# Twelve more key gathers of a GRU/AUGRU kernel wait for a state of the recurrence before they are issued

## The chip, the cores and the metric

The kernel runs on one core of a Trainium2 chip. A core has a matrix engine (TensorE, PE in the profile), a vector engine (VectorE, DVE), an activation engine (ScalarE, ACT), a general engine (GpSimd, POOL) and an engine that mostly issues DMAs (SyncE, SP). Each works through its own list of instructions in order and meets the others only through semaphores. GpSimd also issues the indirect DMAs, the gathers by a list of row numbers. Time is the device time of one launch in microseconds (us).

## The reference

A batch of 1024 users has a history of T = 100 items each, with 128 numbers per item, all in float32. A GRU runs over the history and leaves 100 keys per user. An attention network scores every key against the item in question, with a softmax over the unmasked ones. A second recurrence (AUGRU) runs over the keys again; its update gate is scaled by an attention value. The state at each user's own length goes through a small network to one number. The AUGRU is where the change lies:

```python
def augru_step(h, inp):
    x_t, a_t = inp
    ti = jnp.concatenate([h, x_t], axis=-1)
    r = sigmoid(ti @ aug_Wr.T + aug_br)
    u = sigmoid(ti @ aug_Wu.T + aug_bu)
    h_hat = tanh(concatenate([h * r, x_t], axis=-1) @ aug_Wh.T + aug_bh)
    u = a_t[:, None] * u
    h_new = (1.0 - u) * h + u * h_hat
    return (h_new, h_new)
_, aug_seq = scan(augru_step, h0, (swapaxes(keys, 0, 1), att_seq))
attention_feature = take_along_axis(aug_out, idx, axis=1)[:, 0, :]   # idx = length - 1
```

## The kernel before

**Two phases.** The first phase runs the GRU with the attention and the pooling beside it (`gru_phase`, up to about 1400 us of the profile). The second, `augru_phase`, runs the AUGRU over t = 1 to 99. State 0 is worked out at the end of the first phase.

**Two halves.** The users are sorted by length and split into two halves of 512 (i = 0 and i = 1), features on the 128 partitions and users along the free dimension. Users whose sequence has ended drop out, so the columns shrink from 510 at t = 1 to 500 at t = 3, 496 at t = 4 and so on. `half_step(t, i)` does one step of one half, and the halves alternate: while VectorE and ScalarE finish one half, TensorE works on the other.

**One half step.** TensorE first closes the gate ph of the half step before with its r (L1268), then the gates pr and pu of this half step with the state h (L1268), and then opens three gates of the next half step with its keys (L1264: pr, ph, pu). Each is two matmuls. ScalarE takes the sigmoids (L1292, L1293) and the tanh (L1276). VectorE does pu·c (L1298), r = h·pr (L1300), the new h (L1302), pu·attention (L1305) and `rest` = (pu - 1)·h (L1308). `rest` lives in a ring of three buffers.

**The keys.** The first phase stores the keys in HBM in the order of the users as given; the AUGRU needs them in sorted order. They are fetched by gathers on GpSimd (L193 in `load_row`): one gather brings the keys of 32 sorted users for eight steps, 128 rows of 256 numbers, and sixteen gathers bring a half. `READ` splits the steps into stretches: 0 to 3 (stretch 0), then stretches of eight from `FIRST` = 4, 12, 20 and on. `load_key` turns gathered rows into a matmul operand: by TensorE and ScalarE for stretch 0 (L1246, L1247), by VectorE's transposes for the later ones (L1253).

**When gathers are issued.** The rows of stretch 1 for the first half are fetched during the first phase. For the second half, four of sixteen gathers are issued ahead of the loop and the other twelve by the list `due`, three after each of the four half steps of t = 1 and t = 2. From t = 3 on the gathers of stretch 2 and later are spread in the same way. The place in the program alone doesn't hold GpSimd back, since its list runs ahead of the others. What does is `later["pace"]`: where it is set, `load_row` first copies one column of that tensor into the gather's destination (L192), so that the copy waits for the tensor and the gather for the copy. After `half_step` it is a column of `rest`, and in the kernel before it is left empty for t = 1 and t = 2 (`SOON` is 4).

Ahead of these gathers in GpSimd's list stand eight gathers of pooled attention rows (`att_r`, L158).

Of the kernel before, what the change touches and what calls it, by code (L numbers as in the profile page):

```python
# [58 lines left out]
SOON = P // R  # L59
# [26 lines left out]
def kernel(ctx: ExitStack, tc: tile.TileContext, a: dict, out: bass.AP):  # L86
# [67 lines left out]
    later = {}  # L154
# [998 lines left out]
    def augru_phase(pools, widths, alive):  # L1153
# [22 lines left out]
        def bank(name, n=None):  # L1176

            if n is None:
                n = ring.pop(0)
                ring.append(n)  # L1180
            return ps[n].tile([P, HB], F32, tag="g", name=name)
# [7 lines left out]
        def chosen_rows(i, p, lhsT):  # L1189
            nc.tensor.matmul(p, lhsT=lhsT, rhs=chosen[i], start=True, stop=True)  # L1190

        def first_weights(i, p):
            at = att[1, i] = wp.tile([P, HB], F32, name="at", bufs=6)
            nc.scalar.copy(at, p)

        def store_chosen(i, p):
            chosen_rows(i, p[:SOON, :], quad)
            rows_t = wp.tile([P, HB], F32, tag="att_t", name="att_t", bufs=2)
            nc.scalar.copy(rows_t[:SOON, :], p[:SOON, :])
            nc.sync.dma_start(out=att_d[i][:SOON], in_=rows_t[:SOON, :])  # L1200
            for t in range(2, SOON):
                load_att(t, i)

        def mask_weights(i):
            later_rows = sorted_rows[i][:, :, SOON:T]
            nc.vector.tensor_mul(later_rows, later_rows, used_s[:, i])

        def store_weights(i):

            n = T - SOON  # L1210
            p = pa.tile([P, HB], F32, tag="a", name="pw")
            for g in range(GH):
                nc.tensor.transpose(p[:n, ts(g, P)], sorted_rows[i][:, g, SOON:T], ident)
            rows_t = wp.tile([P, HB], F32, tag="att_t", name="att_t", bufs=2)
            nc.vector.tensor_copy(rows_t[:n, :], p[:n, :])
            nc.sync.dma_start(out=att_d[i][SOON:], in_=rows_t[:n, :])
            load_att(SOON, i)

        def load_att(t, i):
            w = widths[t]  # L1220
            if t >= one and i:
                at = att.pop((t, 0))
            else:
                at = wp.tile([P, HB], F32, name="at", bufs=6)
            att[t, i] = at
            if t >= one:
                at = at[:, ts(i, P)]
            nc.sync.dma_start(
                out=at[:, :w], in_=att_d[i][t, :w].partition_broadcast(P)
            )  # L1230

        def load_key(t, i):

            q = max(j for j, first in enumerate(FIRST) if first <= t)
            w, m, r = widths[t], t - FIRST[q], rows[q, i]
            if t >= one and i:
                k = keys.pop((t, 0))
            else:
                k = qp.tile([P, HB], F32, name="k3")
            keys[t, i] = k  # L1240
            if t >= one:
                k = k[:, ts(i, P)]
            if q < WHOLE:
                p = pa.tile([P, HB], F32, tag="a", name="pk3")
                for g in range(-(-w // P)):
                    nc.tensor.transpose(p[:, ts(g, P)], r[:, g, ts(m, P)], ident)  # L1246
                nc.scalar.copy(k[:, :w], p[:, :w])  # L1247
            else:
                w, n = -(-w // R), KH // len(r)
                for j, part in enumerate(r):  # L1250
                    u = min(w - j * n, n)
                    if u > 0:
                        nc.vector.transpose(  # L1253
                            k.rearrange("p (k r) -> p k r", r=R)[:, j * n : j * n + u, :],
                            part[:, :u, ts(m, R)],
                        )

        def open_gates(t, i, names=("pr", "ph", "pu"), banks=(None,) * 3):

            k = keys[t, i][:, : widths[t]]  # L1260
            for name, n in zip(names, banks):
                m = {"pr": wr, "ph": wh, "pu": wu}[name]
                p = opened[t, i, name] = bank(name, n)[:, : widths[t]]
                nc.tensor.matmul(p, lhsT=m[:, 1, :], rhs=k, start=True, stop=False)  # L1264

        def close_gate(t, i, name, m, v):
            p = opened.pop((t, i, name))
            nc.tensor.matmul(p, lhsT=m[:, 0, :], rhs=v, start=False, stop=True)  # L1268
            return p

        def open_state(t, i):

            r, u, rest = resets.pop((t, i))
            ph = close_gate(t, i, "ph", wh, r)
            c = wp.tile([P, HB], F32, name="c3")[:, : widths[t]]
            nc.scalar.activation(c, ph, AF.Tanh, bias=later["bh"])  # L1276
            states[i] = u, c, rest, h3[i][:, : widths[t]]

        def half_step(t, i):


            w, h = widths[t], h3[i][:, : widths[t]]
            before, after = ((t - 1, 1), (t, 1)) if i == 0 else ((t, 0), (t + 1, 0))
            if before in resets:
                open_state(*before)
            pr = close_gate(t, i, "pr", wr, h)
            pu = close_gate(t, i, "pu", wu, h)
            if t == 1:
                row = pa.tile([P, HB], F32, tag="a", name="row")
                chosen_rows(i, row, quad[:, 1:2].to_broadcast([P, P]))  # L1290
                open_gates(1, i, ("ph",), (None, LATE_BANKS[2])[1 - i :])
            nc.scalar.activation(pr, pr, AF.Sigmoid, bias=later["br"])  # L1292
            nc.scalar.activation(pu, pu, AF.Sigmoid, bias=later["bu"])  # L1293
            if t == 1:
                first_weights(i, row)
            state = states.pop(1 - i, None)
            if state is not None:
                nc.vector.tensor_mul(state[0], state[0], state[1])  # L1298
            r = wp.tile([P, HB], F32, name="r3")[:, :w]
            nc.vector.tensor_mul(r, h, pr)  # L1300
            if state is not None:
                nc.vector.tensor_sub(state[3], state[0], state[2])  # L1302
            if (t, i) == (1, 1):
                store_chosen(0, bank("spare", SPARE))
            nc.vector.tensor_mul(pu, pu, att.pop((t, i))[:, :w])  # L1305
            rest = wp.tile([P, HB], F32, name="rest")[:, :w]

            nc.vector.scalar_tensor_tensor(  # L1308
                out=rest, in0=pu, scalar=1.0, in1=h, op0=ALU.subtract, op1=ALU.mult
            )  # L1310
            later["pace"] = rest[:, 0:1] if t > SOON - 2 else None
            resets[t, i] = r, pu, rest
            if t == 2:
                mask_weights(i)
            if t == 1:
                load_key(2, i)
            if (t, i) == (1, 0):
                open_gates(1, 1, ("pr", "pu"))
            elif after[0] < min(T, one) and (*after, "pr") not in opened:
                open_gates(*after)  # L1320
            elif after[0] == one < T:
                open_both(one, "pr", "pu", "ph")
            if (t, i) == (1, 1):
                store_chosen(1, pa.tile([P, HB], F32, tag="a", name="spare"))
                load_key(3, 0)
            elif (t, i) == (2, 0):
                load_key(3, 1)
            elif (t, i) == (2, 1):
                store_weights(0)
            elif (t, i) == (3, 0):  # L1330
                store_weights(1)
            if SOON - 2 < t < T - 2:
                load_att(t + 2, i)

            if t == FIRST[1] - 1:
                load_key(t + 1, i)
            if (t, i) == (FIRST[1], 1):
                load_key(t + 1, i)
            if FIRST[1] - 2 < t < T - 2 and (t, i) != (FIRST[1] - 1, 1):
                load_key(t + 2, i)  # L1340
# [5 lines left out]
        def open_both(t, *names):  # L1346

            w = widths[t]
            for name in names:
                p = opened[t, name] = bank(name)  # L1350
                m = {"pr": wr, "ph": wh, "pu": wu}[name]
                nc.tensor.matmul(
                    both(p, w), lhsT=m[:, 1, :], rhs=both(keys[t, 1], w, P),
                    start=True, stop=False,
                )
# [233 lines left out]
        if one < T:  # L1589
            next(final)  # L1590
            c, rest, h = sums.pop(T - 1)
# [108 lines left out]
```

## Time and profile before

| what | us |
|---|---|
| median of 3 runs | 1998.83 (1998.15 to 1998.97) |
| the profiled execution, its own time | 2015.4 |
| its span, first to last instruction | 2013.5 |
| TensorE busy with matmuls | 1982.8 |
| VectorE busy | 1674.2 |
| GpSimd busy | 1262.1 |
| ScalarE busy | 940.4 |

The profile is of one execution, which isn't one of the timed runs. In the rows of a timeline the columns are the start in us, the duration in us, the engine, the line of the kernel, the operation, the output and its inputs, the shape, the count, and in brackets how long the engine had been idle and what it waited for. In a row of windows the numbers after the stretch and its length are the busy time of PE, PEld (weight loads), DVE, ACT and POOL, then the granted TensorE clock (1.00 is full), the share of the DMA engines and GB/s. The ends of matmuls are modelled, and the starts are recorded.

### The profile page before, as it was taken

What the parts mean: (1) busy time and instruction counts of PE and PEld (TensorE: products, weight loads), DVE (VectorE), ACT (ScalarE), POOL (GpSimd) and SP (SyncE); (2) the same over time, 40 slices, a digit from 0 to 9 for tenths busy, and PEclk for the clock granted to TensorE, in tenths of its full rate; (3) what the DMA queues carried; (4) which work ended last, traced back from release to release, by engine and by line L of the source; (5) the groups of instructions that cost most, each with busy time, mean ns of one, the idle gap of its engine ahead of it and who ended that gap; (6) DMA issues with size and microseconds to landing.
All of it is one profiled execution on the core that took longest, in us unless ns stands there. A gap on an engine that the chain in (4) does not pass through costs nothing.

```text
span 2013.5 us, 40927 instructions
## 1 busy us (share of the span) xinstructions
PE 1982.8 (98%) x15324; PEld 875.7 (43%) x15324; DVE 1674.2 (83%) x3036; ACT 940.4 (47%) x1689; POOL 1262.1 (63%) x1300
## 2 busy tenths in 40 slices
PE   9999999999999999999999999999699999999998
PEld 2333333333333333333333333334244556678997
DVE  7888998887888897888888898998477777888885
ACT  4445444444445454445445454455234444445553
POOL 0333939569796959495987767989553354445331
PEclk9999999999999999999999999999899999999999
DMA  4443333323334334333432333332443333333331
GB/s 124 98 117 100 98 107 107 105 84 90 107 115 108 108 117 122 109 115 105 126 101 80 99 107 92 107 107 83 126 136 93 95 110 98 94 104 95 81 81 35
DMA packets 244572, 205.59 MB, mean 102 GB/s; under 512 B 61811, under 2 KB 207068, under 8 KB 244364
## 3 DMA queue, kind: packets, MB, share of 16 engines
q1 hardware_dynamic: 231852, 170.31, 29.9%
q0 software_dynamic: 12224, 32.05, 5.7%
q8 instruction: 122, 2.00, 0.4%
q14 instruction: 86, 0.70, 0.1%
q10 hardware_dynamic: 288, 0.52, 0.1%
HBM read 146.75 MB, written 54.42 MB: 100 GB/s over the span
## 4 chain that ended last, share of the span: by engine, by line
PE 93%; DVE 2%; POOL 2%; another core or an unknown queue 1%; ACT 1%; issue 1%; DMA 0%; SPq 0%; DVEq 0%; ACTq 0%; POOLq 0%
PE ps L588 48%; PE pm L770 17%; PE ph L1268 4%; PE pr L1268 4%; PE pu L1268 4%; PE ph L1264 4%; PE pr L1264 4%; PE pu L1264 4%; POOL pooled L700 1%; PE last L737 1%; POOL kw L699 1%; PE pr L1359 0%; PE ph L1359 0%; POOL hist L574 0%
## 5 line engine op out<-in xcount | busy, mean ns | idle before, releaser
L588 PE MATMUL ps<-x,wih 128*32 128x512 f32 x4800 | 601.9, 592 | 0.0
L588 PE MATMUL ps<-hn,whh 128*32 128x512 f32 x4752 | 596.8, 592 | 0.0
L588 PEld LDWEIGHTS ps<-x,wih 128*32 128x32 f32 x4800 | 174.4, 110 | 342.6 <-issue 337.9
L588 PEld LDWEIGHTS ps<-hn,whh 128*32 128x32 f32 x4752 | 172.8, 110 | 339.1 <-issue 337.0
L600 ACT ACTIVATE r<-ps,brz 128x512 f32<-128x512 f32 x200 | 137.5, 687 | 381.9 <-PE ps L588 381.7
L573 POOL TENSOR_TENSOR xm<-x,m 128x512 f32<-128x512 f32 x200 | 233.5, 1168 | 66.9 <-DMA m<-mask_d 66.6
L574 POOL TENSOR_TENSOR hist<-hist,xm 128x512 f32<-128x512 f32 x200 | 257.7, 1288 | 15.7
L193 POOL DMA_INDIRECT rows<-keys_d,idx_k x218 | 211.9, 972 | 85.2 <-POOL rows L192 49.7
L700 POOL TENSOR_TENSOR pooled<-pooled,kw 128x512 f32<-128x512 f32 x192 | 245.0, 1276 | 15.0
L699 POOL TENSOR_TENSOR kw<-kt,e 128x512 f32<-128x512 f32 x192 | 206.3, 1074 | 69.0 <-DVE e L888 69.0
L621 ACT ACTIVATE ps<-ps,bih 128x512 f32<-128x512 f32 x198 | 131.1, 662 | 229.8 <-DVE ps L618 228.7
L770 PE MATMUL pm<-hn,wk 128*32 128x512 f32 x1200 | 214.9, 592 | 0.0
L770 PE MATMUL pm<-kq,wkq 128*32 128x512 f32 x1200 | 214.8, 592 | 0.0
L1276 ACT ACTIVATE c<-ph,bh 128x510 f32<-128x510 f32 (+57 forms) x174 | 88.1, 506 | 254.5 <-PE ph L1268 222.1
L608 DVE SCALAR_TENSOR_TENSOR u<-ps,bhh,r 128x512 f32<-128x512 f32 x198 | 147.5, 745 | 68.8 <-PE ps L588 66.6
L770 PE MATMUL pm<-mv,w 128*32 128x512 f32 (+1 forms) x808 | 194.9, 592 | 1.0 <-DVE e L869 1.0
L192 POOL COPY rows<-rest 128x1 f32<-128x1 f32 x186 | 34.9, 188 | 209.5 <-DVE rest L1308 205.5
L631 DVE TENSOR_TENSOR d<-hn,ps 128x512 f32<-128x512 f32 x198 | 136.1, 687 | 35.9 <-ACT ps L621 35.5
L618 DVE TENSOR_TENSOR ps<-ps,u 128x512 f32<-128x512 f32 x200 | 140.0, 700 | 25.2 <-remote 4.1
L632 DVE TENSOR_TENSOR d<-ps,d 128x512 f32<-128x512 f32 x198 | 136.9, 691 | 26.1 <-ACT ps L622 11.1
L642 ACT COPY hn<-ps 128x512 f32<-128x512 f32 x198 | 115.5, 583 | 91.6 <-DVE kq L637 89.9
L1298 DVE TENSOR_TENSOR pu<-pu,c 128x510 f32<-128x510 f32 (+57 forms) x173 | 81.8, 473 | 89.7 <-ACT c L1276 62.9
(271 smaller groups left out, 3141.3 us busy)
## 6 DMA issues: line engine op xcount, KB each, us to landing
x<-in_hist_x SPq DMA_DIRECT2D x210, 256.0 KB
keys_d<-kt SPq DMA_DIRECT2D x48, 1024.0 KB
m<-mask_d SPq DMA_DIRECT2D x200, 128.0 KB
rows<-keys_d,idx_k POOLq DMA_INDIRECT x218
s_b<-mv SPq DMA_DIRECT2D x200, 8.0 KB
keys_d<-kt SPq DMA_DIRECT2D x32, 64.0 KB
mask_i<-in_mask SPq DMA_DIRECT2D x8, 200.0 KB
part_d<-part SPq DMA_DIRECT2D x2, 400.0 KB
```

The lines of the kernel that those rows point to most:

```text
L193: nc.gpsimd.indirect_dma_start(out=r[:, at, :], out_offset=None, in_=keys_d[q], in_offset=bass.IndirectOffsetOnAxis(ap=idx_k[:, k, i : i + ...
L573: nc.gpsimd.tensor_mul(d, x, m)
L574: nc.gpsimd.tensor_add(acc, acc, d)
L588: nc.tensor.matmul(p[ts(q, R), :], lhsT=w[:, g, ts(q, R)], rhs=v, start=(j == 0), stop=(j == len(parts) - 1),)
L600: nc.scalar.activation(r, pr, AF.Sigmoid, bias=brz[:, 0:1])
L608: nc.vector.scalar_tensor_tensor(out=u, in0=ph, scalar=bhh[:, 2:3], in1=r, op0=ALU.add, op1=ALU.mult,)
L618: nc.vector.tensor_add(pi, pi, u)
L699: eng.tensor_mul(d, k, w)
L700: eng.tensor_add(acc, acc, d)
L770: nc.tensor.matmul(p[i][s, :], lhsT=w[:, s], rhs=v, start=start, stop=stop)
L1264: nc.tensor.matmul(p, lhsT=m[:, 1, :], rhs=k, start=True, stop=False)
L1268: nc.tensor.matmul(p, lhsT=m[:, 0, :], rhs=v, start=False, stop=True)
```

## The change

The exception for t = 1 and t = 2 is taken out:

```diff
@@ half_step @@
             nc.vector.scalar_tensor_tensor(
                 out=rest, in0=pu, scalar=1.0, in1=h, op0=ALU.subtract, op1=ALU.mult
             )
-            later["pace"] = rest[:, 0:1] if t > SOON - 2 else None
+            later["pace"] = rest[:, 0:1]
             resets[t, i] = r, pu, rest
```

On GpSimd the place is the run of sixteen gathers behind the att_r gathers (`rows_14796` is their destination, `keys_d1` the HBM tensor of stretch 1; DMASW names are semaphores of the gathers). Before, they stand one behind the other:

```order
L158 DMA att_r_14791<-pooled_d_80,idx_88 128x128 [waits DMASW7_49]
L193 DMA rows_14796<-keys_d1_61,idx_k_89 128x256 [waits DVE_49,DMASW0_49,PE_49,Activation_49]
L193 DMA rows_14796<-keys_d1_61,idx_k_89 128x256 [waits DMASW1_49]
L193 DMA rows_14796<-keys_d1_61,idx_k_89 128x256 [waits DMASW2_49]
L193 DMA rows_14796<-keys_d1_61,idx_k_89 128x256 [waits DMASW3_49]
L193 DMA rows_14796<-keys_d1_61,idx_k_89 128x256 [waits DMASW4_49]
L193 DMA rows_14796<-keys_d1_61,idx_k_89 128x256 [waits DMASW5_49]
```

In the changed kernel the same place reads (`rest_14814` is that of step 1, first half, `rest_14860` that of step 1, second half):

```order
L193 DMA rows_14796<-keys_d1_61,idx_k_89 128x256 [waits DMASW3_49]
L192 COPY rows_14796<-rest_14814 128x1 [waits DVE_49]
L193 DMA rows_14796<-keys_d1_61,idx_k_89 128x256 [waits DMASW4_49,Pool_49]
L192 COPY rows_14796<-rest_14814 128x1
L193 DMA rows_14796<-keys_d1_61,idx_k_89 128x256 [waits DMASW5_49,Pool_49]
L192 COPY rows_14796<-rest_14814 128x1
L193 DMA rows_14796<-keys_d1_61,idx_k_89 128x256 [waits DMASW6_49,Pool_49]
L192 COPY rows_14796<-rest_14860 128x1 [waits DVE_49]
L193 DMA rows_14796<-keys_d1_61,idx_k_89 128x256 [waits DMASW7_49,Pool_49]
```

The first four gathers stay as they are; each of the other twelve has a copy ahead of it, three copies for each of the four half steps.

On VectorE the place is the half step of t = 3, second half, where the gathered rows are first used. Before:

```order
L1305 TENSOR_TENSOR pu_14974<-pu_14974,at_14879 128x500 [waits DMAHW2_49,Activation_49]
L1308 SCALAR_TENSOR_TENSOR rest_15013<-pu_14974,h_all_93 128x500 [waits DVE_49]
L1253 STREAM_TRANSPOSE k3_15023<-rows_14796 128x512 [waits DMASW4_49,DMASW5_49,DMASW3_49,DMASW6_49,DMASW2_49,DMASW7_49,DMASW1_49,DMASW0_49]
L1298 TENSOR_TENSOR pu_14974<-pu_14974,c3_15030 128x500 [waits Activation_49]
L1300 TENSOR_TENSOR r3_15037<-h_all_93,pr_15015 128x496 [waits Activation_49]
```

And in the changed kernel:

```order
L1305 TENSOR_TENSOR pu_14986<-pu_14986,at_14882 128x500 [waits DMAHW2_49,Activation_49]
L1308 SCALAR_TENSOR_TENSOR rest_15025<-pu_14986,h_all_93 128x500 [waits DVE_49,Pool_49]
L1253 STREAM_TRANSPOSE k3_15035<-rows_14796 128x512 [waits DMASW4_49,DMASW3_49,DMASW5_49,DMASW2_49,DMASW6_49,DMASW1_49,DMASW7_49,DMASW0_49,Pool_49]
L1298 TENSOR_TENSOR pu_14986<-pu_14986,c3_15042 128x500 [waits Activation_49]
L1300 TENSOR_TENSOR r3_15049<-h_all_93,pr_15027 128x496 [waits Activation_49]
```

The order is the same. L1308 and L1253 also wait for GpSimd: L1308 because its buffer is one that copies have read (the same new wait stands at the L1308 of t = 2, second half, and t = 3, first half), L1253 because the copies write into its input. Apart from this no instruction of any engine has moved.

## Prediction

> **What bounds the kernel now.** I read the page first: which engine is full, and what the chain that ended last consists of.
>
> ```profile
> PE 1982.8 (98%) x15324; PEld 875.7 (43%) x15324; DVE 1674.2 (83%) x3036; ACT 940.4 (47%) x1689; POOL 1262.1 (63%) x1300
> PE 93%; DVE 2%; POOL 2%; another core or an unknown queue 1%; ACT 1%; issue 1%; DMA 0%; SPq 0%; DVEq 0%; ACTq 0%; POOLq 0%
> ```
>
> TensorE sets the time. Work on another engine costs nothing until TensorE has to wait for it, and then it costs the wait. Only 2013.5 - 1982.8 = 30.7 us of the span are without a matmul. So I looked next at the timeline of the AUGRU's first steps, where the changed gathers stand, TensorE first:
>
> ```profile
> 1432.64 0.60 PE L1246 MATMUL pk<-ident,rows 128*128 128x128 f32 x4
> ...
> 1436.46 1.00 PE L1264 MATMUL ph<-k,wh 128*128 128x500 f32 x2
> 1447.14 2.04 PE L1264 MATMUL pu<-k,wu 128*128 128x500 f32 x2 [9.68 <-issue]
> ...
> 1453.43 2.05 PE L1268 MATMUL ph<-r,wh 128*128 128x506 f32 x2 [3.40 <-DVE r L1300]
> ...
> 1458.49 1.00 PE L1264 MATMUL pr<-k,wr 128*128 128x500 f32 x2
> 1459.33 1.00 PE L1264 MATMUL ph<-k,wh 128*128 128x500 f32 x2
> ...
> 1463.96 0.99 PE L1264 MATMUL pr<-k,wr 128*128 128x496 f32 x2
> ```
>
> This is the largest hole of the profiled execution, and it lies just beside the changed gathers. From an opening of ph to the next opening of pr, half a step on, the undisturbed rows need 1463.96 - 1459.33 = 4.63 us. So after the ph at 1436.46 the pr of step 3, second half, was due at 1441.09; it came at 1458.49. The hole costs 17.4 us: 9.68 + 3.40 of waiting, the rest by a slow clock. On ScalarE one sees what was late:
>
> ```profile
> 1430.29 0.66 ACT L1293 ACTIVATE pu<-pu,bu 128x506 f32<-128x506 f32 x1
> 1442.90 0.57 ACT L1247 COPY k<-pk 128x500 f32<-128x500 f32 x1 [11.95 <-remote]
> 1446.41 0.68 ACT L1276 ACTIVATE c<-ph,bh 128x506 f32<-128x506 f32 x1 [2.93 <-remote]
> 1452.00 0.66 ACT L1292 ACTIVATE pr<-pr,br 128x506 f32<-128x506 f32 x1 [4.92 <-remote]
> ```
>
> The copy at 1442.90 waits for the transposes of 1432.64 alone, which by their row end at 1433.24. It started 9.7 us after that. The next two were late in the same way, so that the bank for pu came free late. No gather is an input of these three instructions. Now the times: the profiled execution took 2015.4 us, the median of the runs is 1998.83, 16.6 less. Without the hole only 30.7 - 13.1 = 17.6 us without matmuls are left in the whole span, start and tail included, and nearly all of it would have to vanish to make 16.6. The hole itself, 17.4, fits. I therefore read it as belonging to the recorded execution and not to the timed ones, and lay out the timed schedule by taking 17.4 us off every row behind it.
>
> [...]
>
> **The change part by part.** GpSimd's own rows, before and after the hole:
>
> ```profile
> 1428.34 0.94 POOL L158 DMA_INDIRECT att_r<-pooled_d,idx  x1 [0.30 <-issue]
> 1429.58 0.95 POOL L193 DMA_INDIRECT rows<-keys_d,idx_k  x1 [0.30 <-issue]
> ...
> 1433.33 0.95 POOL L193 DMA_INDIRECT rows<-keys_d,idx_k  x1 [0.30 <-issue]
> 1434.58 0.95 POOL L193 DMA_INDIRECT rows<-keys_d,idx_k  x1 [0.30 <-issue]
> ...
> 1448.34 0.94 POOL L193 DMA_INDIRECT rows<-keys_d,idx_k  x1 [0.30 <-issue]
> 1460.99 0.18 POOL L192 COPY rows<-rest 128x1 f32<-128x1 f32 x1 [11.71 <-DVE rest L1308]
> 1461.71 0.98 POOL L193 DMA_INDIRECT rows<-keys_d,idx_k  x1 [0.53 <-POOL rows L192]
> 1462.69 0.20 POOL L192 COPY rows<-rest 128x1 f32<-128x1 f32 x1
> 1463.16 0.98 POOL L193 DMA_INDIRECT rows<-keys_d,idx_k  x1 [0.27 <-POOL rows L192]
> 1464.14 0.19 POOL L192 COPY rows<-rest 128x1 f32<-128x1 f32 x1
> ```
>
> - *How many.* The first four of the sixteen gathers are issued ahead of the loop, when there is no state to wait for. Twelve change, from the one at 1434.58 on.
> - *The waits.* The copies wait, three each, for the state rows (rest) of steps 1 and 2:
>
> ```profile
> 1416.23 0.69 DVE L1308 SCALAR_TENSOR_TENSOR rest<-pu,h_all 128x510 f32<-128x510 f32 x1
> 1421.53 0.69 DVE L1308 SCALAR_TENSOR_TENSOR rest<-pu,h_all 128x510 f32<-128x510 f32 x1
> 1432.11 0.69 DVE L1308 SCALAR_TENSOR_TENSOR rest<-pu,h_all 128x506 f32<-128x506 f32 x1
> ...
> 1454.82 0.69 DVE L1308 SCALAR_TENSOR_TENSOR rest<-pu,h_all 128x506 f32<-128x506 f32 x1
> ...
> 1460.15 0.68 DVE L1308 SCALAR_TENSOR_TENSOR rest<-pu,h_all 128x500 f32<-128x500 f32 x1
> ```
>
> GpSimd is held back by the eight att_r gathers and is free for the first changed copy at 1434.3. By then the first three states are there (1416.9, 1422.2, 1432.8). The fourth, recorded at 1454.82 + 0.69 = 1455.5, is due at 1438.1 without the hole, and its copies come up after nine gathers, at about 1447. So in the timed runs no copy waits: this part costs 0.
> - *The copies themselves.* With no wait, a gather with its copy goes from 1461.71 to 1463.16, 1.45 us; without one, (1448.34 - 1429.58)/15 = 1.25. Twelve times 0.20 is 2.4 us more on GpSimd. At the upper end each group's first copy costs what it does behind a real wait (1460.99 to 1461.71, 0.72, for 0.47), four times 0.25, and the delay is 3.4. I take 2.4, since nothing is waited for.
> - *When the rows land.* The last gather ends its issue at 1449.28. In the DMA view of 1448 to 1452 us (forty slices of 0.1 us) the last traffic is in the slice from 1450.6:
>
> ```profile
> DMA  3000000958567000000299426610000000000000
> ```
>
> So the sixteenth lands at about 1450.7 now, and at 1450.7 + 2.4 = 1453.1 after the change.
> - *Who needs them.* VectorE transposes all sixteen at once for step 4, second half, and TensorE opens that step's gates with the result:
>
> ```profile
> 1466.03 0.68 DVE L1308 SCALAR_TENSOR_TENSOR rest<-pu,h_all 128x500 f32<-128x500 f32 x1
> 1466.76 0.71 DVE L1253 STREAM_TRANSPOSE k<-rows 128x512 f32<-128x512 f32 x1
> 1468.20 0.69 DVE L1298 TENSOR_TENSOR pu<-pu,c 128x500 f32<-128x500 f32 x1 [0.73 <-ACT c L1276]
> 1469.00 0.67 DVE L1300 TENSOR_TENSOR r<-h_all,pr 128x496 f32<-128x496 f32 x1
> ...
> 1468.95 0.99 PE L1264 MATMUL pr<-k,wr 128*128 128x496 f32 x2
> ...
> 1471.45 0.99 PE L1268 MATMUL ph<-r,wh 128*128 128x496 f32 x2
> ```
>
> The transpose ended at 1467.47, 1.48 us ahead of its matmul. Taking 17.4 off, it would start at 1449.36 and could start as late as 1449.36 + 1.48 = 1450.84 before TensorE waits. Now the rows land at 1450.7, just inside: before, the wait of VectorE is covered. At 1453.1 they are 1453.1 - 1450.84 = 2.3 us late, and TensorE is idle for that. Behind the transpose in VectorE's queue stand the product for h, r and h of step 4; r was done at 1469.67 for a ph at 1471.45, and since the opened gates shift as well, this adds nothing to the 2.3.
> - *The new wait on VectorE.* Three of the L1308 now wait until GpSimd has copied from the buffer that they overwrite (a ring of three). The last copies of the first three states end, at 1.45 each from 1434.3, at 1437.4, 1441.7 and 1446.1. The L1308 of (2,1), (3,0) and (3,1) are due at 1437.4, 1442.8 (1460.15 - 17.4) and 1448.6. Only the first is close, and VectorE has next to wait for a tanh there. Cost 0, at most some tenths.
> - *Later gathers* start 2.4 us later and serve step 12, eight steps on: 0. No DMA is added; TensorE's, ScalarE's and SP's queues keep their order.
>
> The sum: against the profiled execution 2015.4 - 17.4 + 2.3 = 2000.3; against the median 1998.83 + 2.3 = **2001.1 us**, which I take, because the first leans on my 17.4 as well. Bounds for the term: 0.5 (rows landing or matmul by 1.8 us better placed in the timed runs) to 3.9 (3.4 of delay and no cover), so 1999.3 to 2002.8.
>
> **The rivals.**
> - *Nothing moves.* If VectorE reaches the transpose some 2 us later in the timed runs than my shifted rows have it, the late rows are covered: 1998.8. For it: the cover of 1.48 is from one execution, and the 17.4 from a subtraction; 17.4 against 16.6 is an error of 0.8 already. Against: the sixteen gathers follow pooled_d alone, whose time doesn't hang on the hole.
> - *Slower, by the clock.* The place is the same transpose. The granted clock reacts to a long hole:
>
> ```profile
> 1440.00:1445.00 5.00, 0.00 (x0) 0.00 (x0) 0.00 (x0) 0.57 (x1) 3.78 (x5) 0.63 0.36 104
> 1450.00:1460.00 10.00, 6.60 (x11) 2.93 (x11) 6.15 (x10) 3.30 (x5) 0.00 (x0) 0.58 0.13 39
> ```
>
> 0.63 over 5 us is 1.3 us at full and the rest at half speed, so the clock fell at 1441.3, 3.8 us after the last matmul ended at 1437.46. 0.58 over 10 us puts its return at 1458.4, 5.0 us after TensorE had steady work again at 1453.43. If the rows come 3.8 us late, at 1454.6 (a paced gather of 1.57 us instead of 1.45), TensorE loses 3.8 and half of 5.0: 1998.8 + 6.3 = 2005.1. For it: 1.57 is not far from 1.45. Against: three paced gathers in a row never took that in the rows above. [...]
> - *Faster: the hole is in every execution and comes from gathers issued without a pause.* Then pacing may close it: 1998.8 - 17.4 = 1981.4. For it: the hole ends 2.7 us after GpSimd's run of gathers, and the paced stretch behind has none. Against: the late start on ScalarE goes back to 1433.3, ahead of the first changed instruction at 1434.3; and the timed runs have no room for it.
> - *The change doesn't pace at all.* That is my own forecast for the waits; only the copies' time remains.
>
> **How the numbers follow.** Late keys without a fall of the clock 0.55 (0.07 of it above 4 us), nothing moves 0.22, the clock 0.13, faster 0.10. About 0.2%, 4 us, is what a measurement can tell from no change: slower 0.07 + 0.13 = 0.20, same 0.48 + 0.22 = 0.70, faster 0.10. The range, 1996 to 2006, takes in the clock's case and a scatter of 2 us below no change; outside are the faster case and a few chances above.
>
> **What would show it.** Right: twelve copies of L192 ahead of 1454, spaced 1.45 us with their gathers and without idle time, and the transpose of the 128x512 rows waiting for the last gather's DMA, with a hole of 1 to 4 us at L1264 pr of 128x496. If the long hole comes again in the recorded execution, the last three copies wait for the fourth state instead, and the recorded time says little. Wrong: a time below 1995 (the hole was real and pacing closed it), copies that do wait in an undisturbed record, or L1308 held by GpSimd.

## The result, and the profile after

| | median, us | range, us | runs |
|---|---|---|---|
| before | 1998.83 | 1996.03 to 2001.15 | 9 |
| changed | 2002.25 | 2001.89 to 2004.80 | 9 |

The changed kernel is slower by 3.4 us: ratio 1.0022, 95% interval 1.0011 to 1.0032. The forecast was 2001.1, with 1996 to 2006 as its range.

Kernels that are compared ran on one chip, with their own runs of the kernel before beside them. Different comparisons got different chips, and here that matters, so each is named: A is the chip of the table, and B, C and D, the second to the fourth, are those of the experiments.

The page of the changed kernel, its busy times with the numbers of instructions and its chain that ended last:

```profile
PE 1980.0 (99%) x15324; PEld 877.6 (44%) x15324; DVE 1673.0 (84%) x3036; ACT 940.0 (47%) x1689; POOL 1264.4 (63%) x1312
...
PE 96%; POOL 1%; DMA 1%; issue 1%; DVE 1%; ACT 0%; POOLq 0%; ACTq 0%; DVEq 0%
```

And the first row of the view of waits for TensorE (total us, times, longest):

```profile
PE pr L1264 <- DVE k L1253: 5.9, 1, 5.9
```

GpSimd has twelve instructions more, and TensorE still sets the end. The span is 1999.8 us instead of 2013.5 (the execution's own time 2001.89): the long hole of the record before is not in this one, and the largest wait is now the one for the transposed keys. GpSimd's timeline (start, duration, engine, line, operation; in brackets the idle time before and what ended it) shows the last unpaced gather, the first copy, and the twelfth paced gather, the sixteenth of the run:

```profile
1433.44 0.94 POOL L193 DMA_INDIRECT rows<-keys_d,idx_k  x1 [0.30 <-issue]
1434.38 0.20 POOL L192 COPY rows<-rest 128x1 f32<-128x1 f32 x1
1434.85 0.97 POOL L193 DMA_INDIRECT rows<-keys_d,idx_k  x1 [0.27 <-POOL rows L192]
1435.82 0.20 POOL L192 COPY rows<-rest 128x1 f32<-128x1 f32 x1
...
1450.68 0.97 POOL L193 DMA_INDIRECT rows<-keys_d,idx_k  x1 [0.27 <-POOL rows L192]
```

No copy waits, and gather and copy take 1.44 us together. VectorE's timeline of the same stretch, with the states and the transpose of the gathered rows, and TensorE's behind it:

```profile
1437.67 0.69 DVE L1308 SCALAR_TENSOR_TENSOR rest<-pu,h_all 128x506 f32<-128x506 f32 x1
...
1443.20 0.68 DVE L1308 SCALAR_TENSOR_TENSOR rest<-pu,h_all 128x500 f32<-128x500 f32 x1
...
1448.73 0.68 DVE L1308 SCALAR_TENSOR_TENSOR rest<-pu,h_all 128x500 f32<-128x500 f32 x1
1456.89 0.71 DVE L1253 STREAM_TRANSPOSE k<-rows 128x512 f32<-128x512 f32 x1 [7.48 <-DMA rows<-keys_d,idx_k]
...
1450.76 1.00 PE L1268 MATMUL pu<-h_all,wu 128*128 128x496 f32 x2
1457.65 2.02 PE L1264 MATMUL pr<-k,wr 128*128 128x496 f32 x2 [5.90 <-DVE k L1253]
...
1464.19 0.99 PE L1264 MATMUL pr<-k,wr 128*128 128x492 f32 x2
```

The transposes do wait for the last gather, but 7.48 us long, and TensorE is idle for 5.90 us. The gather ended its issue at 1451.65 and the transpose that waits for its rows started at 1456.89, 5.2 us later, where I had put 1.4. The windows of the place (busy times, clock, DMA share, GB/s), and in the second fence SyncE's timeline (seven loads of attention rows, `at`, from 1448.20 on), say what else went on:

```profile
1450.00:1455.00 5.00, 1.75 (x5) 0.49 (x3) 0.00 (x0) 1.97 (x3) 3.90 (x8) 1.00 1.00 278
1455.00:1460.00 5.00, 2.35 (x3) 1.18 (x4) 3.08 (x6) 0.00 (x0) 3.30 (x5) 0.72 0.46 153
```

```profile
1448.20 18.23 SPq L1228 DMA_DIRECT2D at<-att_d  x7
```

All DMA engines are full for 5 us. An idle time of 5.90 us can't all be new if the whole change costs 3.4: on this chip the kernel before must have lost part of it already, unless the rest of the two schedules differs.

### The profile page after: what moved, and what is told of

Its sections match the earlier page's. It is cut to its first block, busy times and chain, and to the rows that moved or that the text cites. A ratio compares the mean times of both kernels' runs of the same rounds, so it can differ in the third digit from the quotient of the medians.

```text
span 1999.8 us, 40955 instructions
## 1 busy us (share of the span) xinstructions
PE 1980.0 (99%) x15324; PEld 877.6 (44%) x15324; DVE 1673.0 (84%) x3036; ACT 940.0 (47%) x1689; POOL 1264.4 (63%) x1312
## 4 chain that ended last, share of the span: by engine, by line
PE 96%; POOL 1%; DMA 1%; issue 1%; DVE 1%; ACT 0%; POOLq 0%; ACTq 0%; DVEq 0%
PE ps L588 51%; PE pm L770 18%; PE ph L1268 4%; PE pr L1264 4%; PE ph L1264 4%; PE pu L1264 4%; PE pu L1268 4%; PE pr L1268 4%; POOL rows L193 1%; DMA rows<-keys_d,idx_k 1%; PE last L737 1%; PE pr L1359 0%; PE ph L1359 0%; PE p L1479 0%; ACT pr L1378 0%
```

## The experiments

Two things were to be told apart. **Late landing**: rows land late beside the attention loads, and the copies make them later. **The hole**: what the 17.4 us of the record before are, which I had called an accident of that execution.

### The hole again, on chip B

Three kernels, and a new record of the kernel before. The first edit keeps the copies and takes their wait away (they read a tensor that has long been ready, `quad`, for t = 1 and 2); the others let the attention loads have three buffers instead of six, with and without the change.

```diff
# ready_copies, on the changed kernel
-            later["pace"] = rest[:, 0:1]
+            later["pace"] = rest[:, 0:1] if t > SOON - 2 else quad[:, 0:1]
# ring3_after and ring3_before, on the changed kernel and on the one before
-            at = att[1, i] = wp.tile([P, HB], F32, name="at", bufs=6)
+            at = att[1, i] = wp.tile([P, HB], F32, name="at", bufs=3)
+            if i == 0:
+                for _ in range(3):
+                    wp.tile([P, HB], F32, name="at_pad", bufs=3)
...
-                at = wp.tile([P, HB], F32, name="at", bufs=6)
+                at = wp.tile([P, HB], F32, name="at", bufs=3)
```

The expectations:

> The kernel before, unchanged, for a second profiled execution. The hole of 17.4 us at the AUGRU's step 2 is not in it if it belonged to the one recorded execution, and the profiled time is then near 1999 us. Theory A (my prediction's reading of before): the sixteen gathers land at about 1450.7, the transpose of step 4, second half, starts by 1450.8, and TensorE does not wait at the pr of 128x496. Theory B (the DMA engines are full of attention loads when the last gathers land, in both kernels): the hole at that pr, 7.6 us of lost time in the changed kernel, is there already, and about 7.6 - 3.4 = 4.2 us are lost.

> The changed kernel, but for steps 1 and 2 the copies read a column that has been in memory since the first phase, so that they exist and wait for nothing, and VectorE's three new waits on GpSimd are gone. Theory A: waits cost nothing, the copies' 12 x 0.2 us on GpSimd are all, so the time is that of the changed kernel, +3.4 us on before (within 1). Rival (the waits on the states, or VectorE's waits for the copies, cost time): nearer to before, +0 to +1.5 us.

> The changed kernel with a ring of three buffers for the attention rows instead of six (three dead buffers keep the memory as it is), so that SyncE cannot issue the loads for steps 5 and 6 in one burst at 1448 to 1452 us. Theory B: the last gather, issued by 1451.7, lands at about 1453.5 instead of 1456.8, 4.5 to 5 of the 7.6 us lost at that place come back, and the time is 1997 to 1998.5 us. Theory A without contention: the landing does not change, 2002.3 us.

> The kernel before with the same ring of three. Theory B: its last gather, issued by 1449.3, lands at 1451 to 1452, at most 1.2 us are lost, and the time is 1995 to 1996 us; the changed kernel's loss against it is then the copies' 2.4 us alone. Theory A: nothing was late in the kernel before, so 1998.8 us.

| chip B | median, us | ratio to before |
|---|---|---|
| before, 27 runs | 2017.78 (2014.60 to 2021.87) | |
| ready_copies | 2014.84 | 0.9984 (0.9974 to 0.9993) |
| ring3_after | 2014.65 | 0.9982 (0.9973 to 0.9991) |
| ring3_before | 2018.25 | 0.9997 (0.9988 to 1.0006) |

All four expectations had been worked out for a chip without the hole; ready_copies, for one, was expected 3.4 us above the kernel before. On this chip no run of the kernel before is under 2014.6 us. The new record of it, ScalarE's timeline, then TensorE's with its return and the first opening of step 4 (pr of 128x496), then the start of the sixteenth gather (`remote` stands for another core or a queue that the profile doesn't know):

```profile
1443.17 0.58 ACT L1247 COPY k<-pk 128x500 f32<-128x500 f32 x1 [12.73 <-remote]
...
1432.13 0.60 PE L1246 MATMUL pk<-ident,rows 128*128 128x128 f32 x4
...
1448.80 2.03 PE L1264 MATMUL pu<-k,wu 128*128 128x500 f32 x2 [11.85 <-ACT c L1276]
...
1464.81 0.99 PE L1264 MATMUL pr<-k,wr 128*128 128x496 f32 x2
...
1447.81 0.95 POOL L193 DMA_INDIRECT rows<-keys_d,idx_k  x1 [0.30 <-issue]
```

It is the same hole in the same place: a copy starts 10.4 us after the transposes that it alone waits for have ended (1432.73). So it was no accident of one record. With ready copies the copy, TensorE's return and the opening read:

```profile
1442.57 0.58 ACT L1247 COPY k<-pk 128x500 f32<-128x500 f32 x1 [12.09 <-remote]
...
1446.14 2.03 PE L1264 MATMUL pu<-k,wu 128*128 128x500 f32 x2 [9.16 <-ACT c L1276]
...
1461.96 0.99 PE L1264 MATMUL pr<-k,wr 128*128 128x496 f32 x2
```

TensorE resumes 2.66 us sooner, step 4 opens 2.85 us sooner, and the median falls by 2.9: twelve copies of 0.2 us that wait for nothing shorten the hole. The return alone doesn't tell its price. The clock is at half for 20.5 us in the record of the kernel before, for 17.1 with ready copies and for 17.1 in that of ring3_before (added up from windows of 1 us); there TensorE returns as late as 1451.04 and yet opens step 4 at 1464.79, like the kernel before. Nor does one record size a gain here: the recorded execution of ready_copies took 2018.45 us, the longest of its eleven runs. With the ring of three the time of the kernel before doesn't change. Late landing can't be tested on this chip, since behind the hole the rows have long landed.

### The change itself where the hole is, and a run of gathers cut short, on chip C

The changed kernel unchanged (after_again), the kernel before (before_third), the ring again, and the kernel before with the later twelve gathers left out:

```diff
# four_gathers, on the kernel before (in load_rows)
+        less = q == 1 and i == 1
+        if less:
+            nc.gpsimd.memset(some[0], 0.0)
         for k in range(-(-width // R)):
-            load_row(q, i, k)
+            if not less or k < P // R:
+                load_row(q, i, k)
```

> The changed kernel, unaltered, beside the kernel before on a chip of its own. The first comparison had before at 1998.8 us and no long hole in the changed kernel's record; the later runs had before at 2017.8 us, and every record of theirs has the hole of 17 us. Theory C: the sign depends on whether the hole is there. Without it (before near 1999 us): +2.5 to +4.5 us, as first measured. With it (before near 2018 us): the last three copies wait for the state that the hole delays, the run of gathers pauses and the hole ends sooner, so 2 to 5 us faster than before. Rival: the change costs its copies in both cases, +2 to +4 us.

> The kernel before, for one more record. Without the hole: theory B expects the transpose of the 128x512 rows to wait for the last gather, whose landing is put off by the attention loads, and some 4 us lost at the pr of 128x496; theory A expects no wait of TensorE there. With the hole: the last late signal to ScalarE comes 2 to 4 us after GpSimd's sixteenth gather, as in the four records so far.

> The changed kernel with three instead of six buffers for the attention rows. Without the hole, theory B: the last gather lands at about 1453.5 instead of 1456.8 us, and the time is 4 to 5 us below that of the changed kernel; theory A: the same time as the changed kernel. With the hole: the same as the changed kernel within 1.5 us, since the rows are long there when they are needed.

> The kernel before without the twelve later gathers of the second half's first stretch: their rows are zeros, written by GpSimd ahead of the first four gathers, so a part of the keys of steps 4 to 11 is left out of the computation. It has no late landing and no run of sixteen. Without the hole: theory B expects before's loss at the pr of 128x496 to vanish, 1994 to 1996 us; theory A 1998.8. With the hole: if the run of gathers makes it, it is gone or shrinks to a few us, 2000 to 2005 us; if it comes from something else in these steps, it stays, 2013 to 2018 us.

| chip C | median, us | ratio to before |
|---|---|---|
| before, 21 runs | 2011.96 (2009.54 to 2015.67) | |
| after_again (the change) | 2009.64 | 0.9989 (0.9980 to 0.9998) |
| ring3_after_two | 2008.77 | 0.9983 (0.9974 to 0.9992) |
| four_gathers | 1997.43 | 0.9926 (0.9911 to 0.9941) |

The same change that costs 3.4 us on chip A gains 2.3 us here. The kernel before on this chip, TensorE's return and opening of step 4, and the start of the sixteenth gather:

```profile
1445.34 2.04 PE L1264 MATMUL pu<-k,wu 128*128 128x500 f32 x2 [8.94 <-ACT c L1276]
...
1462.12 0.99 PE L1264 MATMUL pr<-k,wr 128*128 128x496 f32 x2
...
1447.31 0.95 POOL L193 DMA_INDIRECT rows<-keys_d,idx_k  x1 [0.30 <-issue]
```

And the changed kernel: TensorE's return and opening, GpSimd's ninth paced gather and the copy behind it, and the transpose of the gathered rows:

```profile
1442.47 2.03 PE L1264 MATMUL pu<-k,wu 128*128 128x500 f32 x2 [6.20 <-ACT c L1276]
...
1455.83 0.99 PE L1264 MATMUL pr<-k,wr 128*128 128x496 f32 x2
...
1445.16 0.97 POOL L193 DMA_INDIRECT rows<-keys_d,idx_k  x1 [0.27 <-issue]
1449.61 0.44 POOL L192 COPY rows<-rest 128x1 f32<-128x1 f32 x1 [3.47 <-DVE rest L1308]
...
1458.70 0.70 DVE L1253 STREAM_TRANSPOSE k<-rows 128x512 f32<-128x512 f32 x1
```

The hole is shorter (TensorE returns 2.87 us sooner and opens step 4 6.3 us sooner, with the clock at half for 10.2 us instead of 17.1), the tenth copy waits because the hole delays its state, and the transpose waits for nothing: the hole covers the late rows. The two executions' own times differ by 4.4 us (2014.07 and 2009.64), the medians by 2.3, so one pair of records doesn't size this gain either. With four gathers there is no hole. The row of ScalarE that stood at 1441 to 1443 in the records of the kernel before, and the transpose:

```profile
1433.64 0.57 ACT L1251 COPY k<-pk 128x500 f32<-128x500 f32 x1 [2.32 <-PE pk L1250]
...
1449.60 0.70 DVE L1257 STREAM_TRANSPOSE k<-rows 128x512 f32<-128x512 f32 x1
```

So with this edit the hole is gone, and the time is 14.5 us lower. But the edit also puts a memset of 3.5 us (1429.65 to 1433.18) ahead of the four gathers and so breaks the run, just where the first late signal falls: in the kernel before on this chip the late copy was due at 1432.18, ahead of the first gather that the edit leaves out, at 1433.56. The pause may therefore matter as much as the number; that wasn't run by itself.

### Where there is no hole, on chip D

Two of the unpaced gathers moved ahead of the att_r gathers, where GpSimd is idle for 2.46 us (two_ahead_after); the same with the ring of three (ring3_two_ahead); and ten of the sixteen gathers (ten_gathers, the edit of four_gathers with `k < 10`).

```diff
# two_ahead_after, on the changed kernel
-        sorted_rows = [gather_weights(i) for i in range(NH)]
         ahead = load_rows(1, 1, widths[FIRST[1]], kp)
-        for _ in range(P // R):
+        for _ in range(2):
+            next(ahead)
+        sorted_rows = [gather_weights(i) for i in range(NH)]
+        for _ in range(P // R - 2):
             next(ahead)
```

> The kernel before, recorded beside the next runs. If this chip has the hole: the copy of k at 1440 to 1444, the first half-steps of t = 3 some 17 us late. If it has none (time about 1999): the transpose of the 128x512 rows waits for the last gather, since the attention loads start at about 1446 and the rows then land 3 to 6 us after their issue ends at 1449.3; by my prediction's landing of 1.4 us the transpose waits for nothing.

> The changed kernel with two of the four unpaced key gathers put ahead of the att_r gathers, into the 2.46 us in which GpSimd is idle there. All later gathers end 2.5 us sooner, the last at about 1449.2 without a hole. Without a hole on this chip: the landing beside the attention loads decides, rows at about 1454, so 2 to 4 of the 7.6 us that the changed kernel loses are back and the ratio to before is 0.999 to 1.001. With the hole: if it lasts as long as the run of gathers, 2.5 us less of it, ratio about 0.9975 to 0.998; if pacing alone decided, as the changed kernel, 0.999.

> The same with the attention loads held back by a ring of three buffers instead of six. Without a hole: if the loads are what makes the rows land late, the rows land 1.4 us after their issue, nothing waits, and the 7.6 us are gone: about 1994.6, ratio 0.998; if they are not, as the run with two gathers ahead. With the hole: 0.997 (the ring was worth 0.06% more than the change alone on the third chip).

> The kernel before with ten of the sixteen gathers (the other rows are memset to zero, so part of the keys of steps 4 to 11 is left out). The run of gathers ends at about 1441.8 instead of 1449.3. With the hole: if it lasts as long as the run, it is about 7.5 us shorter (ratio 0.996, the copy of k at 1437 to 1441); if the hole needs a full run of more than some 26 gathers, it is gone (0.9925, as with four gathers); if it is set off by any gather beyond the fourth and then has its own length, it stays (1.000). Without a hole: ratio 0.998, since the rows land before the attention loads.

| chip D | median, us | ratio to before |
|---|---|---|
| before, 25 runs | 1998.45 (1996.21 to 2001.34) | |
| two_ahead_after | 1998.51 | 1.0000 (0.9991 to 1.0010) |
| ring3_two_ahead | 1997.04 | 0.9994 (0.9984 to 1.0003) |
| ten_gathers | 1993.34 | 0.9974 (0.9964 to 0.9985) |

Chip D has no hole, and so gave the record that I had lacked: the kernel before without it (its own time 1997.1). The sixteenth gather, VectorE's last state and transpose, and TensorE:

```profile
1446.73 0.95 POOL L193 DMA_INDIRECT rows<-keys_d,idx_k  x1 [0.30 <-issue]
...
1446.79 0.68 DVE L1308 SCALAR_TENSOR_TENSOR rest<-pu,h_all 128x500 f32<-128x500 f32 x1
1451.73 0.71 DVE L1253 STREAM_TRANSPOSE k<-rows 128x512 f32<-128x512 f32 x1 [4.27 <-DMA rows<-keys_d,idx_k]
...
1448.88 0.99 PE L1268 MATMUL pu<-h_all,wu 128*128 128x496 f32 x2
1452.50 1.93 PE L1264 MATMUL pr<-k,wr 128*128 128x496 f32 x2 [2.63 <-DVE k L1253]
...
1459.29 0.99 PE L1264 MATMUL pr<-k,wr 128*128 128x492 f32 x2
```

The kernel before waits for these rows too. Lay it beside the changed kernel's record (of chip A; the changed kernel has none on D), with the zero of both at the same row, L1308 of 128x500 (1446.79 and 1448.73, so 1.94 apart). The sixteenth gather starts 3.95 - 1.94 = 2.01 us later, the transpose 5.16 - 1.94 = 3.22 later, TensorE's idle time is 5.90 instead of 2.63, 3.27 more, and the opening of step 5 (the row of 128x492) comes 4.90 - 1.94 = 2.96 us later. That is the change's price, and the runs of chip A say 3.4. From issue to transpose are 5.00 us before and 6.21 after: 2.0 us of the lateness are the copies' and 1.2 the longer landing.

What the kernel before loses here is seen from ten_gathers:

```profile
1448.31 0.68 DVE L1312 SCALAR_TENSOR_TENSOR rest<-pu,h_all 128x500 f32<-128x500 f32 x1
1449.07 0.71 DVE L1257 STREAM_TRANSPOSE k<-rows 128x512 f32<-128x512 f32 x1
...
1456.22 0.99 PE L1268 MATMUL pr<-k,wr 128*128 128x492 f32 x2
```

No wait, and from the state row to the opening of step 5 are 7.91 us instead of 12.50. That is 4.6 us, and the time is 5.1 lower. Now the landing, beside loads from six buffers (two_ahead_after) and from three (ring3_two_ahead): sixteenth gather, transpose, TensorE, first for six,

```profile
1446.79 0.97 POOL L193 DMA_INDIRECT rows<-keys_d,idx_k  x1 [0.27 <-DVE pu L1305]
...
1452.73 0.71 DVE L1253 STREAM_TRANSPOSE k<-rows 128x512 f32<-128x512 f32 x1 [5.31 <-DMA rows<-keys_d,idx_k]
...
1453.50 2.02 PE L1264 MATMUL pr<-k,wr 128*128 128x496 f32 x2 [3.73 <-DVE k L1253]
```

In the first, the two gathers moved ahead have just paid for the copies: the sixteenth starts at 1446.79, as in the kernel before (1446.73), and the time is that of the kernel before. Then for three:

```profile
1447.66 0.97 POOL L193 DMA_INDIRECT rows<-keys_d,idx_k  x1 [0.27 <-DVE pu L1308]
...
1451.93 0.71 DVE L1256 STREAM_TRANSPOSE k<-rows 128x512 f32<-128x512 f32 x1 [3.64 <-DMA rows<-keys_d,idx_k]
...
1452.70 1.11 PE L1267 MATMUL pr<-k,wr 128*128 128x496 f32 x2 [2.07 <-DVE k L1256]
```

From issue to transpose are 5.94 us with six buffers and 4.27 with three. Nothing else differs in the code, so the loads do hold the rows back, by some 1.7 us in these two records. But they are not all of it: I had expected the rows 1.4 us after their issue's end, and they took about 3.3. The time, 0.9994, can't be told from no change, and no kernel here that computes everything beats the kernel before where there is no hole.

## Why the prediction was right, and where its steps were wrong

**Right, as forecast.** The places and sizes on GpSimd: twelve copies, none waiting, 1.44 us per gather (forecast 1.45), the sixteenth gather 2.0 us later (forecast 2.4; one gather of the kernel before on chip D took 1.33 us instead of 0.95, which makes most of the difference). The wait of the three L1308 cost nothing: their rows carry no idle time. The states came where the rows less 17.4 us had them: their ends at 1438.4, 1443.9 and 1449.4, against 1438.1, 1443.4 and 1449.3. The delay ends at the named instruction, the transpose of 128x512 rows, and TensorE's new idle time is at the named opening.

**The term that was mis-sized: when the rows land.** "So the sixteenth lands at about 1450.7 now", 1.4 us after its issue's end, was read from the record with the hole, in which no attention load was near. Without the hole they follow at once, and the rows took 4.1 us before and 5.2 after. Hence "just inside: before, the wait of VectorE is covered" was wrong: the kernel before already lost 4.6 us there. The sum came out near all the same, because it is a difference. With no cover left, the whole delay reaches TensorE (3.22 us at the transpose, 3.27 at TensorE), 1.2 of it by the longer landing: 2.0 + 1.2 = 3.2 instead of 2.3. The timed 3.4 lies inside the bounds of 0.5 to 3.9, though the terms named for the upper one, 3.4 of delay and no cover, make 3.4. That the sum came so near is in part luck: the clock's price happens to be nearly the same in the two records laid side by side, and in that of two_ahead_after it is over 1 us higher (below). And 4 us as the least that a measurement can tell was too coarse: the interval here is 2.2 to 6.4 us, so that 3.4 is told from no change.

**The step that was wrong: the hole as an accident of the recorded execution.** The subtraction of 17.4 us gave the right schedule for chips A and D. But my grounds, that no gather is an input of the late instructions and that the timed runs leave no room, held for chip A's times alone. On chips B and C every run of the kernel before is 11 to 23 us longer than chip A's median, the records there have the hole, and with the edit of four_gathers it goes. On which chip the execution of the profile before ran isn't on record: its 2015.4 us lie among the times of B and C, and no timed run on A is above 2001.15. So it may have come from another chip than the median beside it. Recording alone isn't what makes the hole: the records of the changed kernel on A and of the kernel before on D have none.

**The rivals.** "Nothing moves" needed cover for late rows, and there was none. "Faster: the hole is in every execution and comes from gathers issued without a pause" had the gathers right where the hole exists, as far as four_gathers shows, and its price wrong: pacing takes 2.3 us off, not 17.4. The copies there are mostly ready and first wait after nine gathers. That the last three copies then wait for the fourth state was forecast, and seen (3.47 us). "Slower, by the clock" had the place, but not that the kernel before pays it too: its windows around the wait on chip D, one us each,

```profile
1452.00:1453.00 1.00, 0.50 (x1) 0.41 (x2) 1.00 (x3) 0.00 (x0) 0.72 (x3) 0.81 1.17 346
1453.00:1454.00 1.00, 1.00 (x2) 0.34 (x1) 1.00 (x3) 0.00 (x0) 0.72 (x3) 0.50 0.65 232
...
1456.00:1457.00 1.00, 1.00 (x4) 0.53 (x3) 0.16 (x1) 0.00 (x0) 0.76 (x1) 0.98 0.67 181
```

put the fall at 1452.62 (0.81 is 0.62 us at full and the rest at half) and the return at 1456.04. So the fall costs half of 3.4 us, 1.7, here. In the changed kernel's record TensorE is still idle for the first 0.5 us of the slow stretch, so it costs 1.5 there, and nearly drops out of the difference. It needn't: with two gathers ahead the clock stayed at half twice as long, 5.7 us of it with TensorE at work, which costs 2.8.

**What stays open.** What delays the signals between TensorE and ScalarE during a run of gathers, and why two chips show it and two don't; whether it is the chip or its state at that time these runs can't tell. Ten gathers were meant to show whether the hole lasts as long as the run, but met a chip without it. And of the landing, the 4.3 us that are left with three buffers aren't explained.

## What to carry to other kernels

A landing time that was read with no load beside it was a lower bound here (1.4 us after the issue, against 3.3 to 5.2 beside loads): look at what else is issued in the same stretch of the schedule that will be timed, and whether the transfer already sets a wait there. When a record differs from the timed runs by the length of one hole, say only that the two differ, and get a second record before giving the hole a cause. Pacing copies cost their own time on the engine that issues (1.44 us per gather instead of 1.25 here), so they belong where the transfers have room to be late.

## What the runs showed of the hardware

- **Signals late during a run of gathers.** With 32 gathers on GpSimd and one pause among them (2.46 us in the first record of the kernel before), the copy on ScalarE started 10.4 us after the end of the transposes that it waits for (chip B). With the last twelve left out and 3.5 us of pause ahead of the four before them it came at once (chip C). On chip D the same gathers went without the delay (TensorE was busy for 19.87 of the 20 us from 1430 to 1450), and the times on chip A leave no room for it.
- **The hole reacted to small spacing.** A copy of 0.2 us ahead of each of twelve gathers, with no wait, made the time 2.9 us shorter (0.9984, chip B).
- **The clock's slow stretches were near multiples of 3.4 us in these records.** The stretch was 3.42 us in the record of chip D above. In the changed kernel's the clock fell 5.4 us after the last matmul's end (1451.76), at 1457.18, and came back at 1460.58, 3.40 us on, by the rows

```profile
1457.00:1458.00 1.00, 0.35 (x1) 0.35 (x2) 1.00 (x2) 0.00 (x0) 0.72 (x3) 0.59 0.16 62
...
1460.00:1461.00 1.00, 1.00 (x3) 0.48 (x2) 1.00 (x3) 0.00 (x0) 0.18 (x1) 0.71 0.12 44
```

With two gathers ahead the stretch was twice that: by the rows

```profile
1450.00:1455.00 5.00, 1.50 (x2) 0.83 (x3) 2.27 (x4) 0.51 (x1) 4.13 (x7) 0.73 0.79 281
1455.00:1460.00 5.00, 5.00 (x8) 2.07 (x7) 2.12 (x5) 0.07 (x1) 2.51 (x5) 0.58 0.38 104
```

2.7 and 4.2 us at half, 6.9 together. In the records with the hole on B and C the windows add up to 10.2 us (after_again), 17.1 (ready_copies, ring3_before, before_third) and 20.5 (before_again), three, five and six times 3.4. The start was less regular: in the kernel before on chip D the clock fell 2.75 us after the last matmul's end (1449.87), in the changed kernel 5.4. My 3.8 and 5.0 were single readings.
